# Layer 0 of two outlook-attention layers: the outer weight rows are shifted by the table's transfer instead of by TensorE

## The chip, the cores and the metric

The kernel runs on one core of one Trainium2 chip. The metric is the device time of one execution in microseconds (us); lower is better. The kernel before takes 3531.84 us, the median of three runs (3530.87 to 3535.32).

The engines go by the profile's names: PE is TensorE (matmuls), PEld its weight loads, DVE is VectorE, ACT is ScalarE, POOL is GpSimd, SP is SyncE, which here only issues transfers.

## The reference

The input x is 8 images of 56 x 56 pixels with 384 channels, in float32. Two layers follow one another, each of the form x + layer(groupnorm(x)). The change touches only layer 0:

```python
v = jnp.einsum('bhwc,oc->bhwo', x, Wv)
a = jnp.einsum('bhwc,oc->bhwo', x, Wa).reshape(b, n, heads, k2, k2)
attn = jax.nn.softmax(a * d ** (-0.5), axis=-1)
out = jnp.einsum('bnhpq,bnqhd->bnphd', attn, v_unf).reshape(b, h, w, k2, c)
canvas = canvas.at[:, i:i + h, j:j + w].add(out[:, :, :, p])   # for each p = (i, j)
```

There are 12 heads and a 3 x 3 window (k2 = 9). Every pixel makes a 9 x 9 matrix of weights for each head: the softmax runs over the nine neighbours q that are read, and there are nine target positions p that the result is added to. Reading and adding together connect a pixel with the pixels up to two rows and two columns away. So per head an output pixel has 5 x 5 summed weights, each made of several attention weights that were computed at different pixels. Layer 1 is simpler (6 heads, one weight for each of nine neighbours).

## The kernel before, in words

**Tiling.** The kernel works on two images at a time (a "pair", four of them). One column of a pair is 2 x 56 = 112 pixels, one pixel for each partition (R = 112). Layer 0 runs over 4 x 56 = 224 columns; a loop step handles one column for the first stages and earlier columns for the later ones. Seven columns make a patch, and there are 32 patches.

**A column in layer 0.** `attend` computes the logits in three groups of 288 (three matmuls each), DVE subtracts the maximum (L550, L551), ACT takes the exponential (Exp, L555), DVE makes the denominators (L567 to L573; L573 also multiplies with `inside`, which is zero where a weight would leave the image), and POOL multiplies (L574). The v projection follows; ACT copies it out (L562) and issues its transfers into a table `vtab0` in DRAM. `presum`, two steps later, adds the weights of three neighbouring columns on POOL into `pre`: for each of nine (pi, qi), and for each of five column offsets f and 12 heads, one number. `fold`, three steps after `attend`, sums over rows.

**The fold.** Five row offsets e = pi - qi + 2 from 0 to 4 are wanted. A weight that was computed at row r belongs to another row, one up or one down, when qi is 0 or 2. So `fold` multiplies `pre` with `shift[:, qi, :]`, a 112 x 112 matrix of zeros and ones that moves each row by one, once for qi = 0 and once for qi = 2, into a PSUM tile `pw` of 5 x 60 numbers. Each matmul takes all three pi at once, 180 columns. Offset e = 0 has one term only (pi 0, qi 2), and e = 4 one term only (pi 2, qi 0); for both ACT copies `pw` to the tile `wt` (L619). For e = 1, 2, 3 DVE adds the unshifted qi = 1 part (L620). Then ACT issues one transfer of `wt`, 112 partitions x 5 rows of 84 numbers, into a table `ztab0` (L625); for four of seven columns the column belongs to two patches, and there are two transfers. `wt` exists twice and `pre` twice.

**The patch.** After the last column of a patch, SP fetches the table `ztab0` and the v table back in another layout (`z` and `vp`). Four steps later PE contracts them (`pc`, L664 copies them out on ACT), then multiplies with the output weights (`po`). These come as jobs that are slipped between a column's matmuls, so of seven columns two have contractions, three have output projections and two have neither.

**What sets the order.** PE's and some others' instructions are kept in program order. The framework's scheduler sets the order of the rest, ACT's and DVE's above all, when the program is built. [...] Before a table is first used, `clear_weights` fills its margins with zeros (SP, L201).

Of the kernel before, what the change touches and what calls it, by code (L numbers as in the profile page):

```python
# [9 lines left out]
AF = mybir.ActivationFunctionType  # L10
# [5 lines left out]
def two_outlook_layers(  # L16
# [32 lines left out]
    nc = tc.nc  # L49
# [5 lines left out]
    R = IMG * H  # L55
    MARGIN = 2
# [8 lines left out]
    PX = 7  # L65
    NPX = W // PX
# [5 lines left out]
    K, K2 = 3, 9  # L72
    E0 = 2 * K - 1
# [9 lines left out]
    ROW0 = HEADS0 * PX  # L83
# [13 lines left out]
    LINE0, LINE1 = SX0 * SLOT0 + ROW0, SX1 * SLOT1 + ROW1  # L97
    NTAB = 3
# [11 lines left out]
    ztab0 = [dram.tile([RT + 1, LINE0], F32, name=f"ztab0_{n}") for n in range(NTAB)]  # L110
# [7 lines left out]
    def matmul(*args, **kwargs):  # L118
        tc.keep_in_program_order(nc.tensor.matmul(*args, **kwargs))  # L119
# [48 lines left out]
    shift = const.tile([R, K, R], F32, name="shift")  # L168
# [13 lines left out]
    inside = const.tile([R, K, PH_ALL], F32, name="inside")  # L182
# [12 lines left out]
    def fill(table, first, dims, width):  # L195

        src = zeros[: dims[0][1], :width]
        if len(dims) > 1:
            src = src.unsqueeze(1).to_broadcast([dims[0][1], dims[1][1], width])
        tc.keep_in_program_order(  # L200
            nc.sync.dma_start(bass.AP(table.tensor, table.offset + first, [*dims, [1, width]]), src)  # L201
        )
# [12 lines left out]
    def clear_weights(table, line, part, sx, slot, row, first, e, ep):  # L215
        fill(table, 0, [[part, MARGIN * line // part]], part)
        fill(table, (MARGIN + R) * line, [[part, (MARGIN + 1) * line // part]], part)
        top = MARGIN * line
        fill(table, top, [[line, R]], first * row)
        fill(table, top + (first + e) * row, [[line, R], [slot, sx]], (ep - e) * row)  # L220

    def clears():

        yield 3, lambda: clear_v(vtab0, SX0, 2)

        yield 4, lambda: fill(
            ztab0[0], MARGIN * LINE0 + FIRST0 * ROW0, [[LINE0, R], [SLOT0, 2]], E0 * ROW0
        )
        for n, t in enumerate(ztab0):
            yield (5, 2 * PX, 3 * PX)[n], lambda t=t: clear_weights(  # L230
                t, LINE0, 366, SX0, SLOT0, ROW0, FIRST0, E0, EP0
            )
        yield 4 * PX, lambda: clear_v(vtab1, SX1, 1)
        for n, t in enumerate(ztab1):
            yield (5 + n) * PX, lambda t=t: clear_weights(
                t, LINE1, 350, SX1, SLOT1, ROW1, FIRST1, K, EP1
            )
# [59 lines left out]
    def patches_of(col, pad):  # L297

        for px in range(NPX):
            sx = col - PX * px + pad  # L300
            if 0 <= sx < PX + 2 * pad:
                yield px, sx
# [94 lines left out]
    def layer0(late, pools):  # L397
# [209 lines left out]
        def fold(pair, c):  # L607


            pre = pres.pop((pair, c)).rearrange("r (pi qi) f h -> r pi qi (f h)", qi=K)  # L610
            pw = ps.tile([R, E0, E0 * HEADS0], F32, tag="f", name=f"pw_{pair}_{c}")
            for qi in (0, 2):
                matmul(
                    pw[:, 2 - qi : 2 - qi + K, :], shift[:, qi, :], pre[:, :, qi, :],
                    start=(qi == 0), stop=(qi == 2), skip_group_check=True,
                )
            wt = wts[c % NWT]
            mid = wt[:, :, SX0 - E0 : SX0, :].rearrange("r e f h -> r e (f h)")
            nc.scalar.copy(mid[:, 0 : E0 : E0 - 1, :], pw[:, 0 : E0 : E0 - 1, :])  # L619
            nc.vector.tensor_tensor(mid[:, 1 : 1 + K, :], pw[:, 1 : 1 + K, :], pre[:, :, 1, :], ALU.add)  # L620

            for px, sx in patches_of(c, 2):
                lo = SX0 - 1 - sx
                at = sx * SLOT0 + FIRST0 * ROW0
                nc.scalar.dma_start(  # L625
                    ztab0[(pair * NPX + px) % NTAB][MARGIN : MARGIN + R, at : at + E0 * ROW0].rearrange("r (e w) -> r e w", e=E0),
                    wt[:, :, lo : lo + PX, :].rearrange("r e m h -> r e (m h)"),
                )

        def fetch_v(pair, px):  # L630
# [119 lines left out]
        for step in range(NPAIR * W + LAG):  # L750
            if 2 <= step < NPAIR * W + 2:
                presum(*divmod(step - 2, W))
            todo = [lambda: jobs.run(step, 1)] * 2
            if step >= LAG:
                todo.insert(1, lambda: fold(*divmod(step - LAG, W)))
            between = lambda: todo.pop(0)() if todo else None
            if step < NPAIR * W:
                attend(*divmod(step, W), between)
                upkeep(step)
            while todo:  # L760
                between()

            pair, c = divmod(step - LAG - PX, W)
            if pair >= 0 and c % PX == 0:
                fetch_v(pair, c // PX)
            pair, c = divmod(step - LAG - PX - 1, W)
            if pair >= 0 and c % PX == 0:
                fetch(pair, c // PX, step + 4)
# [334 lines left out]
```

## Time and profile before

| what | value |
|---|---|
| median of 3 runs | 3531.84 us |
| the profiled execution, its own time | 3516.74 us |
| its span, first to last instruction | 3514.6 us |
| mean granted TensorE clock | 0.987 |
| layer 0, stretch from 75 to 2320 us | PE busy 2219.82 us, DVE 1524.10, ACT 689.01, POOL 932.48 |
| rest of the span, from 2320 us | PE busy 1155.52 of 1194.60 us |
| fold matmuls `pw` (112 x 180), 896 passes | 174.5 us busy |
| copy L619, 224 times | 58.0 us busy, 259 ns each |
| table transfers from `wt` (L625) | 336, 183.8 KB each, 6.8 us from issue to landing |

Busy time is the time in which an engine executes; issuing a transfer and waiting for a semaphore are not counted. A float32 matmul stands in the profile as two passes, so that a fold's two matmuls are four records. The durations of matmul records overlap; the distance between the starts of neighbours says what one costs. The profiled execution is one run, and the median of others lies some 15 us above it.

### The profile page before, as it was taken

The numbers are of one execution on the slowest core, as the hardware profiler recorded it, in microseconds if no ns is written. First come the engines' busy times: TensorE is split into PE (matmuls) and PEld (weight loads), VectorE is DVE, ScalarE is ACT, GpSimd is POOL, SyncE is SP. The second block draws the span as 40 slices with busy tenths as digits, with TensorE's granted clock in tenths as the row PEclk, the third lists the DMA queues.
The fourth block names the chain that finished last, engine by engine and source line by source line (L and its number), as shares of the span: only waits on it lengthen the run. The fifth ranks groups of instructions, "written<-read, shape, count | busy, mean of one in ns | idle before, by whom it ended". The sixth has DMA issues, their size and how long they took to land. (4 is left out here: it accounts for less than half of the span.)

```text
span 3514.6 us, 72311 instructions
## 1 busy us (share of the span) xinstructions
PE 3427.7 (98%) x29014; PEld 2353.0 (67%) x29014; DVE 1935.8 (55%) x4680; ACT 1173.3 (33%) x2727; POOL 1202.1 (34%) x1833
## 2 busy tenths in 40 slices
PE   7899999999999999999999999988999999999998
PEld 5577777777777777777777777655666666666665
DVE  6666666667666676667766666633333333333331
ACT  4333223333333233333322223223434434343432
POOL 2543434434344344344443444331222222221220
PEclk8999999999999999999999999999999999999998
DMA  8999988688886878887757776676878787878775
GB/s 270 286 288 282 275 275 267 212 256 253 279 263 209 272 221 273 259 252 256 236 181 226 245 225 193 222 271 192 226 221 234 217 229 219 243 205 237 216 219 147
DMA packets 672893, 839.34 MB, mean 239 GB/s; under 512 B 302190, under 2 KB 566574, under 8 KB 668462
## 3 DMA queue, kind: packets, MB, share of 16 engines
q1 hardware_dynamic: 321422, 537.46, 47.9%
q10 hardware_dynamic: 323872, 210.54, 22.7%
q0 software_dynamic: 27264, 86.73, 7.5%
q8 instruction: 228, 3.74, 0.5%
q14 instruction: 107, 0.88, 0.1%
HBM read 512.95 MB, written 321.66 MB: 237 GB/s over the span
## 5 line engine op out<-in xcount | busy, mean ns | idle before, releaser
L119 PE MATMUL bank<-wa_t,xn 128*112 128x288 f32 x4032 | 1086.9, 409 | 11.4 <-ACT v L562 7.8
L574 POOL TENSOR_TENSOR at<-at,den 112x972 f32<-112x972 f32 x224 | 504.6, 2253 | 1193.1 <-DVE den L573 1137.8
L119 PEld LDWEIGHTS bank<-wa_t,xn 128*112 128x112 f32 x4032 | 693.4, 177 | 263.7 <-issue 34.3
L119 PE MATMUL po<-yT,wo_t 128*128 128x448 f32 (+1 forms) x2304 | 817.5, 494 | 5.3 <-DVE x1t L685 4.8
L119 PEld LDWEIGHTS po<-yT,wo_t 128*128 128x128 f32 x2304 | 432.8, 191 | 293.5 <-issue 185.4
L119 PE MATMUL pc<-z,vp 121*32 121x49 f32 (+1 forms) x17664 | 487.9, 254 | 25.3 <-DMA vp<-vtab 10.4
L119 PEld LDWEIGHTS pc<-z,vp 121*32 121x32 f32 (+1 forms) x17664 | 441.3, 131 | 103.3 <-issue 79.5
L550 DVE TENSOR_REDUCE mx<-bank 112x36 f32<-112x324 f32 x672 | 327.6, 487 | 310.6 <-PE bank L119 303.7
L317 POOL DMA_DIRECT2D vtab<-v x392 | 213.1, 547 | 825.3 <-DVE v L132 810.4
L119 PE MATMUL bank<-wc_t,xn 128*128 128x438 f32 x1176 | 478.8, 543 | 5.0 <-DMA wo_t<-in_wo 5.0
L119 PE MATMUL bank<-wv_t,xn 128*128 128x384 f32 x1176 | 417.9, 492 | 0.0
L555 ACT ACTIVATE at<-at 112x972 f32<-112x972 f32 x224 | 227.0, 1014 | 344.9 <-DVE at L551 317.6
L551 DVE TENSOR_TENSOR at<-bank,mx 112x324 f32<-112x324 f32 x672 | 328.8, 489 | 21.1 <-DVE mx L550 0.5
L119 PEld LDWEIGHTS bank<-wc_t,xn 128*128 128x128 f32 x1176 | 214.0, 191 | 174.8 <-issue 162.4
L119 PEld LDWEIGHTS bank<-wv_t,xn 128*128 128x128 f32 x1176 | 219.5, 190 | 139.6 <-issue 18.7
L619 ACT COPY wt<-pw 112x120 f32<-112x120 f32 x224 | 58.0, 259 | 654.0 <-PE pw L119 591.2
L597 POOL TENSOR_TENSOR pre<-at,at 112x108 f32<-112x108 f32 (+1 forms) x440 | 238.0, 541 | 110.4 <-DVE wt L620 96.0
L567 DVE TENSOR_TENSOR d<-at 112x432 f32<-112x432 f32 x224 | 141.7, 632 | 204.7 <-ACT at L555 204.7
L132 DVE TENSOR_TENSOR lgt<-bank,ba_t 128x54 f32<-128x54 f32 x196 | 41.7, 213 | 361.3 <-PE bank L119 361.3
L132 DVE SCALAR_TENSOR_TENSOR x1t<-po,bo_t,x1t 128x448 f32<-128x448 f32 (+1 forms) x156 | 97.7, 626 | 248.9 <-PE po L119 248.9
L664 ACT COPY yT<-pc 128x294 f32<-128x294 f32 x256 | 103.4, 407 | 368.9 <-PE pc L119 325.9
L535 ACT ACTIVATE xn<-xin,bias,scale 128x224 f32<-128x224 f32 x336 | 172.9, 566 | 67.2 <-PE bank L119 36.0
(100 smaller groups left out, 2924.6 us busy)
## 6 DMA issues: line engine op xcount, KB each, us to landing
z<-ztab SPq DMA_DIRECT2D x64, 2352.0 KB, 18.0
vp<-vtab SPq DMA_DIRECT2D x64, 1536.0 KB, 8.3
ztab<-wt ACTq DMA_DIRECT2D x336, 183.8 KB, 6.8
vp<-vtab SPq DMA_DIRECT2D x64, 945.0 KB, 12.0
xres<-xT SPq DMA_DIRECT2D x32, 1176.0 KB, 10.1
xin<-xT ACTq DMA_DIRECT2D x54, 672.0 KB, 7.3
z<-ztab SPq DMA_DIRECT2D x128, 258.4 KB, 4.5
x1t<-x SPq DMA_DIRECT2D x26, 1176.0 KB, 19.0
```

Source lines behind the costliest of these rows:

```text
L119: tc.keep_in_program_order(nc.tensor.matmul(*args, **kwargs))
L132: return lambda *args, **kwargs: tc.keep_in_program_order(op(*args, **kwargs))
L317: queue.dma_start(bass.AP(table.tensor, table.offset + first, [[line, rows], [(R + GAP) * line - PX * C, n], [1, C]],), v.unsqueeze(1).to_ ...
L535: nc.scalar.activation(to[:, i, :, rows], xin[:, i, :, rows], AF.Identity, bias=bias[:, i, b : b + 1], scale=scale[:, i, b : b + 1],)
L550: nc.vector.tensor_reduce(mx[:, pi, :], pl.rearrange("r q a -> r a q"), AX.X, ALU.max)
L551: nc.vector.tensor_tensor(at[:, pi], pl, mx[:, pi, :].unsqueeze(1).to_broadcast([R, K2, PH]), ALU.subtract)
L555: nc.scalar.activation(at, at, AF.Exp, scale=SCALE0)
L567: nc.vector.tensor_add(d4, at[:, :, 0:4], at[:, :, 4:8])
L574: nc.gpsimd.tensor_tensor(at, at, den.unsqueeze(2).to_broadcast([R, K, K2, PH]), ALU.mult)
L597: nc.gpsimd.tensor_tensor(dst, terms[0], terms[1], ALU.add)
L619: nc.scalar.copy(mid[:, 0 : E0 : E0 - 1, :], pw[:, 0 : E0 : E0 - 1, :])
L664: nc.scalar.copy(yT[:, :, :, b, rows_of], pc.rearrange("p i n y m -> p i m (n y)"))
```

## The change

The outer rows, e = 0 and e = 4, are not shifted by a matmul any more. ACT writes them into `wt` at the row where they were computed, with two activations that multiply by `inside[:, qi, 0:1]`, so that a row whose weight belongs to the next image gives zero. The transfer then puts them one row lower (e = 0) or one row higher (e = 4) in the table. It is therefore split in two: one transfer for the three middle rows, one for the two outer ones. The two matmuls take two of the three pi each, 120 columns instead of 180. In each table the two places that no transfer reaches any more, e = 0 of the first row and e = 4 of the last, are filled with zeros at the start; the function that does this serves the tables of both layers.

```diff
+        fill(table, top + first * row, [[slot, sx]], row)
+        fill(table, top + (R - 1) * line + (first + e - 1) * row, [[slot, sx]], row)
...
             for qi in (0, 2):
+                lo = qi // 2
                 matmul(
-                    pw[:, 2 - qi : 2 - qi + K, :], shift[:, qi, :], pre[:, :, qi, :],
+                    pw[:, 2 - qi + lo : 4 - qi + lo, :], shift[:, qi, :], pre[:, lo : lo + 2, qi, :],
                     start=(qi == 0), stop=(qi == 2), skip_group_check=True,
                 )
...
-            nc.scalar.copy(mid[:, 0 : E0 : E0 - 1, :], pw[:, 0 : E0 : E0 - 1, :])
+
+            for e, pi, qi in ((0, 0, 2), (E0 - 1, 2, 0)):
+                nc.scalar.activation(
+                    mid[:, e, :], pre[:, pi, qi, :], AF.Copy, scale=inside[:, qi, 0:1]
+                )
             nc.vector.tensor_tensor(mid[:, 1 : 1 + K, :], pw[:, 1 : 1 + K, :], pre[:, :, 1, :], ALU.add)
...
+                table = ztab0[(pair * NPX + px) % NTAB]
+                first = table.offset + MARGIN * LINE0 + at
+                weights = wt[:, :, lo : lo + PX, :].rearrange("r e m h -> r e (m h)")
+                nc.scalar.dma_start(
+                    bass.AP(table.tensor, first + ROW0, [[LINE0, R], [ROW0, K], [1, ROW0]]),
+                    weights[:, 1 : 1 + K],
+                )
                 nc.scalar.dma_start(
-                    ztab0[(pair * NPX + px) % NTAB][MARGIN : MARGIN + R, at : at + E0 * ROW0].rearrange("r (e w) -> r e w", e=E0),
-                    wt[:, :, lo : lo + PX, :].rearrange("r e m h -> r e (m h)"),
+                    bass.AP(
+                        table.tensor, first + LINE0,
+                        [[LINE0, R], [(E0 - 1) * ROW0 - 2 * LINE0, 2], [1, ROW0]],
+                    ),
+                    weights[:, 0 : E0 : E0 - 1],
                 )
```

## The prediction

> **What bounds the kernel now.** I read the page's totals first, then the stretches of the span, then TensorE's own waits, and last one stretch of the timeline around a fold. The totals and the queues:
>
> ```profile
> span 3514.6 us, 72311 instructions
> PE 3427.7 (98%) x29014; PEld 2353.0 (67%) x29014; DVE 1935.8 (55%) x4680; ACT 1173.3 (33%) x2727; POOL 1202.1 (34%) x1833
> ...
> q1 hardware_dynamic: 321422, 537.46, 47.9%
> q10 hardware_dynamic: 323872, 210.54, 22.7%
> ...
> z<-ztab SPq DMA_DIRECT2D x64, 2352.0 KB, 18.0
> ...
> ztab<-wt ACTq DMA_DIRECT2D x336, 183.8 KB, 6.8
> ```
>
> TensorE (PE) is the bound: 87 us of the span without a matmul. The stretches split that by layer (layer 0 is 75 to 2320 us):
>
> ```profile
> 75.00:2320.00 2245.00, 2219.82 (x19721) 1586.75 (x19719) 1524.10 (x3764) 689.01 (x1357) 932.48 (x1341) 1.00 0.79 248
> ...
> 100.00:300.00 200.00, 185.51 (x1451) 131.56 (x1450) 131.47 (x330) 62.25 (x124) 92.47 (x128) 0.97 0.96 294
> ...
> 700.00:900.00 200.00, 200.00 (x1617) 143.03 (x1616) 140.06 (x359) 63.55 (x124) 82.05 (x120) 1.00 0.85 267
> ```
>
> Columns: length, busy time of PE, weight loads, DVE, ACT, POOL, then granted clock, DMA share, GB/s. In layer 0 PE is busy for 98.9% and in the middle for all of it, at a granted clock of 1.00; only the stretch from 100 to 300 us, with DMA at 0.96, leaves it 14 us idle. So PE work taken from layer 0 is time, unless the change makes PE wait. Who makes ACT wait in the steady part, 300 to 2320 us (total, times, longest):
>
> ```profile
> ACT wt L619 <- PE pw L119: 548.6, 172, 6.3
> ACT yT L664 <- PE pc L119: 285.9, 204, 3.5
> ACT at L555 <- DVE at L551: 273.0, 120, 2.9
> ...
> ACT wt L619 <- DMA vtab<-v: 28.8, 6, 5.3
> ```
>
> ACT mostly waits for PE. Its waits for a DMA come to 79 us over all lines, up to 6.1 us each, and PE has no idle time to match. One fold in the timeline (start, length in us):
>
> ```profile
> 816.91 0.78 PE L119 MATMUL pw<-pre,shift 112*112 112x180 f32 x4
> ...
> 817.52 1.62 PE L119 MATMUL bank<-wa_t,xn 128*112 128x288 f32 x6
> ...
> 817.72 0.26 ACT L619 COPY wt<-pw 112x120 f32<-112x120 f32 x1 [2.99 <-PE pw L119]
> 818.07 0.35 DVE L620 TENSOR_TENSOR wt<-pw,pre 112x180 f32<-112x180 f32 x1
> ...
> 818.45 0.32 ACTq L625 DMA_DIRECT2D ztab<-wt  x1
> ...
> 818.80 0.27 POOL L595 COPY pre<-at 112x108 f32<-112x108 f32 x1
> ...
> 820.77 1.00 ACT L555 ACTIVATE at<-at 112x972 f32<-112x972 f32 x1
> 820.92 0.55 PE L122 MATMUL pt<-ident,xr 112*128 112x112 f32 x4
> ...
> 821.30 3.08 PE L119 MATMUL bank<-wa_t,xn 128*112 128x288 f32 x12
> ...
> 824.21 0.78 PE L119 MATMUL pw<-pre,shift 112*112 112x180 f32 x4
> ```
>
> The four passes of a fold hold PE for 817.52 - 816.91 = 0.61 us. ACT copies when they are done, DVE adds, ACT issues the table's transfer. The POOL copy at 818.80 completes pre of the *next* fold, which PE asks for only at 824.21.
>
> [...] Here the 112-column transposes start every (821.30 - 820.92)/4 = 95 ns with a load each, so a pass of 120 columns is not held up by its load. [...]
>
> **The change part by part.** The sum is against the profiled execution, 3516.7 us with a span of 3514.6; the median shown is 3531.8, 15 us higher, and I carry the difference over.
>
> *PE.* Passes of 180 columns become 120. Rate: 12 passes of 288 columns from 821.30 to 824.21 are 242.5 ns each; with 95 ns for 112 columns that is 0.838 ns a column, so 120 columns take 102 ns. A fold goes from 0.61 to 0.41 us: 0.20 x 224 = 45 us less. If the weight load did hold the pass at the 176 ns that one takes, nothing is gained; the transposes exclude that.
>
> *ACT, outer rows.* One PSUM copy of 259 ns becomes two activations of 60 elements: [...] 0.57 us for both. That is 0.3 us x 224 = 69 us more, on an engine at 689 us of 2245. They wait for pre (POOL), not for PE.
>
> *ACT, issues.* 336 more ztab transfers, each about 0.35 us of ACT's queue (two in a row start 0.35 us apart): 118 us. Packets and bytes stay: 112x5 rows of 336 B become 112x3 and 112x2. The DVE add is unchanged. SP gets 12 small zero fills, of which six lie in layer 0's tables, near the first columns: hidden behind four steps that a patch waits anyway.
>
> *Order.* The built program shows the real edit. In 171 of 224 columns ACT now does the outer rows of fold c, the transfers of them and the middle transfer of fold c-1 *ahead of* Exp of column c+2; before, the copy of c-1 stood there. So a loop closes within one column: Exp (1.02), the denominators on DVE (2.8 bare, about 3.2 with what the new order puts between), POOL's multiply and pre (3.46 from den to pre), the two activations (0.57 and 0.1 of hand-over), two or four issues (0.7 or 1.4), the next Exp. Sum 9.1 us for a column with one table, 9.8 with two (four of seven columns). PE's column is 9.95 us now (224 folds from 82.5 to 2311.5 us) and 9.75 after. The loop just fits on average but not in the two columns of each seven without contraction or projection, about 7.3 us long. From the trace: Exp starts a median 1.2 us after that pre, and needs 1.45 to 2.15 (activations and issues, taken high). It would be late in 57 of the 168 such columns past the start, by 1.6 us on average. Behind it in ACT stand the v copy and xt; behind its result d (L567) in DVE, and then the reduction that frees the bank which the v matmul wants: PE can bear 1.2 to 2 us there in the short columns, 5 to 6 in the others. Most lateness falls where the margin is 5 or more. I take 10 us of PE waits in all; ends: 0, and 57 x 1.6 = 90 if the margins held nothing.
>
> *Semaphores.* [...] 4.97 issues a column look back 8/4.97 x 9.95 = 16 us; 6.47 look back 12 us. ztab's 6.8 us fits; z's 18 does not, and neither do late ones of the others. In the trace 74 of ACT's 730 steady issues stood within the lost 3.7 us of such a wait, worth 141 us of ACT time at most; the half at vtab issues come just after Exp, where ACT goes on to wait for pre anyway. I take 8 us on PE; ends 0 and 47, a third of the 141. Early, where DMA is at 0.96, the 4 us of gain of those 20 columns is not had.
>
> *z.* The middle rows' transfer now follows the next fold's activations: pre of that fold is ready a median 2.2 us after pw starts, where DVE is done after 1.5. So the table is written some 2 us later; z lands 7 to 18 us ahead of its first contraction. Nothing. pre's buffer gets a second reader, ACT, earlier than DVE's add, which POOL waits for already (96 us): nothing.
>
> Sum: -45 + 10 + 8 + 4 = -23: 3494 for the profiled execution, **3509 us** for the median.
>
> **Rivals.** *Full gain:* ACT's slack (689 of 2245 busy) takes everything: 3532 - 45 = 3487. For it, ACT's DMA waits of up to 6 us before cost PE nothing. *Eaten:* waits equal the gain, 3532: the loop's 9.1 to 9.8 us against 9.75 leaves no room for the added semaphore waits. *Slower:* the Exp loop becomes the bound. Place: ACT between POOL's pre and the next Exp; price: each stall of ACT there (z's semaphore, the fourth issue) passes whole into den, pre and the next Exp, as POOL's and DVE's parts can't be hurried; from 0.20 us of PE wait a column on average it decides. At 0.35 us it is 78 - 45 = 33 us slower, 3565. Against it: 53 columns keep the looser order, each time resetting the loop, often at the short columns. *Memory:* DMA's share of 0.79 can't bind, no byte is added.
>
> **Chances.** Partly had (3509) 0.42, full 0.16, eaten 0.15, slower 0.27. A difference within 0.2%, 7 us, can't be told from none. The range holds all but the far slow end: 3484 to 3556; the likeliest case alone 3488 to 3522. Faster 0.58, same 0.15, slower 0.27.
>
> **What would show it.** pw matmuls of 112x120, folds of 0.41 us; ACT's 548.6 us wait for pw gone, a wait for POOL's pre in its place; more ACT waits at ztab and vtab issues. Right if PE's idle time in layer 0 grows from 25 to under 60 us; wrong if "bank" or "pw" waits for DVE or POOL grow past 70 us, or if pc waits for the yT copies that stand behind the new activations.

## The result: 0.14% faster, where 0.65% was forecast

The kernel after takes 3528.64 us (median of 20 runs, 3517.24 to 3542.70), the kernel before on the same chips 3533.18 us (20 runs, 3523.22 to 3541.42). The ratio is 0.9986, with a 95% interval of 0.9975 to 0.9998: a gain of about 5 us, within the 0.2% that count as no difference here. The forecast was -23 us. The profiled execution of after has a span of 3523.7 us, 9 us *more* than the one of before, though after is not slower in the timed runs: single executions of either kernel lie up to some 16 us from their median. So below, totals are taken from the timed ratios, and places from the traces.

The page of after, its totals, two queues, two groups of instructions (busy us, mean ns | idle time ahead of them on their engine, and what ended it) and two transfers:

```profile
span 3523.7 us, 72959 instructions
...
PE 3396.9 (96%) x29014; PEld 2309.1 (66%) x29014; DVE 1915.6 (54%) x4680; ACT 1232.1 (35%) x2951; POOL 1196.8 (34%) x1833
...
q1 hardware_dynamic: 321662, 537.49, 47.7%
q10 hardware_dynamic: 329248, 210.56, 22.3%
...
L626 ACT ACTIVATE wt<-pre,inside 112x60 f32<-112x60 f32 x448 | 133.3, 338 | 796.2 <-POOL pre L598 597.0
L570 DVE TENSOR_TENSOR d<-at 112x432 f32<-112x432 f32 x224 | 140.7, 628 | 415.0 <-ACT at L558 414.2
...
z<-ztab SPq DMA_DIRECT2D x64, 2352.0 KB
...
ztab<-wt ACTq DMA_DIRECT2D x336, 110.2 KB
```

The bytes are those of before, and so nearly is their time. PE has 31 us less busy time, and the span did not follow. The line to look at is L570: DVE, which starts the denominators there, sat idle for 414.2 us until Exp (L558, L555 before) was done. In the page of before the same wait was 204.7 us:

```profile
L567 DVE TENSOR_TENSOR d<-at 112x432 f32<-112x432 f32 x224 | 141.7, 632 | 204.7 <-ACT at L555 204.7
```

Exp comes later than before.

The stretches of after, columns as for before:

```profile
75.00:2320.00 2245.00, 2187.81 (x19720) 1541.74 (x19718) 1504.21 (x3765) 747.79 (x1581) 927.23 (x1341) 0.99 0.78 248
100.00:300.00 200.00, 179.25 (x1442) 125.45 (x1440) 125.08 (x323) 70.03 (x150) 91.95 (x125) 0.97 0.92 287
700.00:900.00 200.00, 199.28 (x1886) 141.94 (x1885) 138.27 (x361) 72.99 (x153) 78.69 (x116) 1.00 0.81 256
```

PE's idle time in layer 0 went from 25 to 57 us. In the early stretch it went from 14 to 21 us in 200, while the share of DMA fell from 0.96 to 0.92. PE's largest waits in layer 0 (75 to 2320 us; total, times, longest) say for what it stood; none of them ends with a transfer:

```profile
PE pw L119 <- POOL pre L598: 18.2, 6, 8.3
PE bank L119 <- DVE at L554: 13.6, 14, 1.4
PE bank L119 <- ACT v L565: 12.3, 9, 4.3
PE pc L119 <- ACT yT L683: 8.8, 9, 2.2
PE po L119 <- DVE x1t L704: 2.4, 2, 1.7
```

Before, these were 10.2, none, 7.8, 2.0 and 0.7 us. No single wait took the gain. POOL, DVE and ACT are each a little late, as they are when a chain that runs through all three is late. ACT's waits in the steady part (300 to 2320 us) show where that chain is tied together:

```profile
ACT wt L626 <- POOL pre L598: 574.2, 143, 7.9
ACT at L558 <- DVE at L554: 147.1, 71, 4.9
ACT yT L683 <- PE pc L119: 136.9, 85, 4.7
ACT wt L626 <- DMA vtab<-v: 96.7, 19, 6.5
ACT wt L626 <- DMA ztab<-wt: 42.8, 9, 6.6
```

Before, ACT waited 548.6 us there for PE's fold; now it waits for POOL's `pre`, ahead of Exp. The two rows of L626 that name a DMA belong to `pre` as well: of the 30 waits of L626 that are put down to a DMA in this stretch, 29 end 0.03 to 0.04 us after the POOL copy (L598) that completes `pre`, as nearly all those that are put down to POOL do. The transfers named there had landed by then. Exp's own wait for its data fell from 273.0 to 147.1 us: ACT more often gets to Exp when the data have long been there. Ahead of Exp some waits for transfers are real: in the three that are put down to a fetch of z (16.8 us in all) Exp starts 7.4, 3.7 and 5.1 us after its last data.

One such case, from the timeline of after (start, length in us):

```profile
902.66 0.27 POOL L598 COPY pre<-at 112x108 f32<-112x108 f32 x1
...
902.97 0.58 ACT L626 ACTIVATE wt<-pre,inside 112x60 f32<-112x60 f32 x2 [4.32 <-POOL pre L598]
903.43 0.49 DVE L554 TENSOR_TENSOR at<-bank,mx 112x324 f32<-112x324 f32 x1
...
907.28 0.31 ACTq L641 DMA_DIRECT2D ztab<-wt  x1
907.64 1.01 ACT L558 ACTIVATE at<-at 112x972 f32<-112x972 f32 x1 [4.09 <-DMA z<-ztab]
...
908.56 0.46 ACT L565 COPY v<-bank 128x384 f32<-128x384 f32 x1
908.68 0.61 DVE L570 TENSOR_TENSOR d<-at 112x432 f32<-112x432 f32 x1 [4.76 <-ACT at L558]
...
909.07 1.71 PE L119 MATMUL bank<-wa_t,xn 128*112 128x288 f32 x6 [0.56 <-ACT v L565]
...
912.20 2.20 PE L119 MATMUL bank<-wv_t,xn 128*128 128x384 f32 x6 [1.42 <-DVE at L554]
...
912.47 2.24 POOL L577 TENSOR_TENSOR at<-at,den 112x972 f32<-112x972 f32 x1 [8.72 <-DVE den L576]
...
915.92 0.58 ACT L626 ACTIVATE wt<-pre,inside 112x60 f32<-112x60 f32 x2 [6.47 <-POOL pre L598]
```

Exp's data are complete at 903.92 (the subtraction of 903.43), but ACT has already done the outer rows of a fold, and their transfer (L641) stands ahead of Exp in its queue; by the profile it waits until a fetch of z has landed. It goes at 907.28, and Exp at 907.64, 3.7 us late. The copy of v is late with it (PE waits 0.56 us), DVE's sums are late (PE waits 1.42 us for the bank), POOL multiplies after 8.72 us of idleness, and `pre` of the next fold is late: ACT, whose next activations need it, waits until 915.92, and the next Exp comes at 916.88. PE lost 2.0 us in this column. It saves 0.2 us in each.

### The profile page after: what moved, and what is told of

It reads as the page before. It is cut to its first block, busy times and chain, and to the rows that moved or that the text cites. A ratio compares the mean times of both kernels' runs of the same rounds, so it can differ in the third digit from the quotient of the medians.

```text
span 3523.7 us, 72959 instructions
## 1 busy us (share of the span) xinstructions
PE 3396.9 (96%) x29014; PEld 2309.1 (66%) x29014; DVE 1915.6 (54%) x4680; ACT 1232.1 (35%) x2951; POOL 1196.8 (34%) x1833
## 4 chain that ended last, share of the span: by engine, by line
PE 59%; DMA 3%; DVE 3%; issue 3%; POOL 2%; ACT 2%; ACTq 1%; POOLq 0%; SPq 0%; DVEq 0%
PE bank L119 30%; PE po L119 15%; PE pc L119 9%; PE pw L119 2%; PE pt L122 1%; POOL at L577 1%; DMA lgtab<-lgt 1%; PE bank L122 1%; ACT at L558 1%; DMA at<-lgtab 1%; DMA z<-ztab 1%; POOL pre L600 1%; DMA vtab<-v 0%; DVE d L570 0%; DVE den L575 0%
## 5 line engine op out<-in xcount | busy, mean ns | idle before, releaser
L119 PEld LDWEIGHTS bank<-wa_t,xn 128*112 128x112 f32 x4032 | 684.2, 178 | 270.7 <-issue 36.8
L119 PE MATMUL bank<-wv_t,xn 128*128 128x384 f32 x1176 | 419.9, 493 | 13.7 <-DVE at L554 13.6
L626 ACT ACTIVATE wt<-pre,inside 112x60 f32<-112x60 f32 x448 | 133.3, 338 | 796.2 <-POOL pre L598 597.0
L570 DVE TENSOR_TENSOR d<-at 112x432 f32<-112x432 f32 x224 | 140.7, 628 | 415.0 <-ACT at L558 414.2
L558 ACT ACTIVATE at<-at 112x972 f32<-112x972 f32 x224 | 226.9, 1013 | 299.8 <-DVE at L554 170.3
L132 ACT COPY ot<-pt 112x384 f32<-112x384 f32 x128 | 61.3, 479 | 389.1 <-PE pt L122 353.6
```

The source lines that it names most:

```text
L132: return lambda *args, **kwargs: tc.keep_in_program_order(op(*args, **kwargs))
L558: nc.scalar.activation(at, at, AF.Exp, scale=SCALE0)
L570: nc.vector.tensor_add(d4, at[:, :, 0:4], at[:, :, 4:8])
L626: nc.scalar.activation(mid[:, e, :], pre[:, pi, qi, :], AF.Copy, scale=inside[:, qi, 0:1])
```

## The experiments

Each ratio is to the kernel before, run on the same chip, with its 95% interval; 0.0010 is 3.5 us. "Behind the full cut" is read from the traces: how much later than in the kernel before the `pw` matmuls of a column start, plus 0.2 us for each column whose fold was already cut. It comes from one profiled execution each. At column 223 it agrees with the timed ratios within some 7 us; e5_semaphores, which costs 2 us in the timed runs, stands 5.8 us behind at column 42 and 8.8 at column 223, so differences of that size can be those of two executions.

My theory, once the result was there: the order of ACT's queue, outer rows ahead of Exp, cost the gain (the loop). The rivals: the split transfers did, by ACT's added issues or by their claims on the completion semaphores (theory B in the expectations; A is the loop); or the cut was never worth 45 us. Of these semaphores the packed trace of before shows this: the 1478 transfers that ACT and SP issue signal eight of them, 184 or 185 times each; one of them comes round after 8 issues (median; in 634 of 1470 cases after exactly 8), and 476 of the issues have a wait for the semaphore that they then signal. In the trace of after it is 1826 transfers, the same eight semaphores, and 630 such waits.

**e1_pe_cut: only PE's part, in the kernel before.**

```diff
             for qi in (0, 2):
+                lo = qi // 2
                 matmul(
-                    pw[:, 2 - qi : 2 - qi + K, :], shift[:, qi, :], pre[:, :, qi, :],
+                    pw[:, 2 - qi + lo : 4 - qi + lo, :], shift[:, qi, :], pre[:, lo : lo + 2, qi, :],
...
-            nc.scalar.copy(mid[:, 0 : E0 : E0 - 1, :], pw[:, 0 : E0 : E0 - 1, :])
+            nc.scalar.copy(mid[:, 0 : E0 : E0 - 1, :], pw[:, 1 : 1 + K : K - 1, :])
```

> The matmul cut alone: 120-column passes, outer rows copied from two middle rows of pw (so the outer weights are not the right ones), one transfer as before. Both theories expect the whole gain of 0.20 us a fold, 45 us, 3488 us (ratio 0.987), since nothing on ACT or in the transfers changes. A ratio above 0.993 would say that the cut itself is worth less than its columns.

Measured: 0.9881 [0.9867, 0.9894], 3481.37 against 3522.82 us. The cut is worth 42 us. The price of a pass was right, and the gain of the early columns is had but for 7.5 us (behind the full cut at column 42; 5.5 us at column 223).

**e2_split_only: only the split transfer, in the kernel before** (the rows stay where they are, the order of ACT too).

```diff
...
+                nc.scalar.dma_start(
+                    bass.AP(table.tensor, first + ROW0, [[LINE0, R], [ROW0, K], [1, ROW0]]),
+                    weights[:, 1 : 1 + K],
+                )
                 nc.scalar.dma_start(
-                    ztab0[(pair * NPX + px) % NTAB][MARGIN : MARGIN + R, at : at + E0 * ROW0].rearrange("r (e w) -> r e w", e=E0),
-                    wt[:, :, lo : lo + PX, :].rearrange("r e m h -> r e (m h)"),
+                    bass.AP(table.tensor, first, [[LINE0, R], [(E0 - 1) * ROW0, 2], [1, ROW0]]),
+                    weights[:, 0 : E0 : E0 - 1],
                 )
```

> The kernel before with the table transfer split in two, rows where they were, nothing else. Theory A (the loop of Exp, den, pre, outer rows, next Exp costs the gain): the order on ACT is the old one, so hardly slower, under 8 us (ratio at most 1.002). Theory B (336 more issues on the eight shared completion semaphores cost the gain): 25 to 40 us slower, ratio 1.007 to 1.011, most of it before 520 us of the span.

Measured: 1.0031 [1.0020, 1.0043]: 11 us slower, more than theory A allowed and far less than theory B asked for. In its trace all of that arises before column 42 (11.9 us later than before there, 8.9 at the end).

**e3_one_transfer: the changed kernel with the one transfer of before.** 151 of 224 columns keep the outer rows ahead of Exp.

```diff
...
                 nc.scalar.dma_start(
-                    bass.AP(table.tensor, first + ROW0, [[LINE0, R], [ROW0, K], [1, ROW0]]),
-                    weights[:, 1 : 1 + K],
-                )
-                nc.scalar.dma_start(
-                    bass.AP(
-                        table.tensor, first + LINE0,
-                        [[LINE0, R], [(E0 - 1) * ROW0 - 2 * LINE0, 2], [1, ROW0]],
-                    ),
-                    weights[:, 0 : E0 : E0 - 1],
+                    ztab0[(pair * NPX + px) % NTAB][MARGIN : MARGIN + R, at : at + E0 * ROW0].rearrange("r (e w) -> r e w", e=E0),
+                    wt[:, :, lo : lo + PX, :].rearrange("r e m h -> r e (m h)"),
                 )
```

> The changed kernel with one unsplit transfer of all five rows to where they were computed (so the outer rows are not moved). The outer rows still stand ahead of Exp in most columns (151 of 224). Theory A: still near 3525 us, ratio 0.996 to 1.000. Theory B: the gain appears, 3490 us, ratio 0.988.

Measured: 0.9930 [0.9917, 0.9944]. Without the split 25 us of the 42 are had, between the two theories: neither the order nor the split takes the gain alone.

**e4_behind_exp: the changed kernel with nothing but the order undone.** The outer rows are held behind the Exp that was issued last; no column has them ahead any more. The split stays.

```diff
-            nc.scalar.activation(at, at, AF.Exp, scale=SCALE0)
+            exps.append(nc.scalar.activation(at, at, AF.Exp, scale=SCALE0).ins)
...
-            for e, pi, qi in ((0, 0, 2), (E0 - 1, 2, 0)):
-                nc.scalar.activation(
-                    mid[:, e, :], pre[:, pi, qi, :], AF.Copy, scale=inside[:, qi, 0:1]
-                )
+            with tc.issue_after(exps[-1]) if exps else nullcontext():
+                for e, pi, qi in ((0, 0, 2), (E0 - 1, 2, 0)):
+                    nc.scalar.activation(
+                        mid[:, e, :], pre[:, pi, qi, :], AF.Copy, scale=inside[:, qi, 0:1]
+                    )
```

> The changed kernel, but the outer rows of column c are held behind Exp of column c+2 on ACT in every column, so the loop never closes within one column; all transfers as in the changed kernel. Theory A: 3490 to 3500 us, ratio 0.988 to 0.991. Theory B: no better than the changed kernel, 3520 to 3530 us, ratio 0.996 to 0.999.

Measured: 0.9904 [0.9891, 0.9918], against 0.9986 of the changed kernel, as theory A expected: with the split in place, the order costs 29 us. DVE's waits from 300 to 2320 us show it, in the kernel before

```profile
DVE mx L550 <- PE bank L119: 265.0, 304, 3.2
DVE d L567 <- ACT at L555: 178.9, 98, 3.7
```

in the changed kernel

```profile
DVE d L570 <- ACT at L558: 356.5, 149, 8.5
DVE mx L553 <- PE bank L119: 148.9, 213, 2.8
```

and in e4_behind_exp:

```profile
DVE mx L553 <- PE bank L119: 240.8, 305, 5.2
DVE d L570 <- ACT at L558: 205.0, 125, 10.5
```

With the order undone DVE waits again mostly for PE's logits, as it did in the kernel before.

**e6_one_behind: both undone**, e3_one_transfer with the hold of e4_behind_exp (the two diffs above together). What is left of the change are the short matmuls and ACT's two activations.

> Outer rows from pre held behind Exp as in the run before, and the transfer unsplit (so the outer rows are not moved): loop and split both gone, the two activations left. If order and split are the whole loss: as the matmul cut alone, 0.9881 within 0.0015. If ACT's added work costs by itself: above 0.991.

Measured: 0.9896 [0.9881, 0.9912], at the edge of what was expected if order and split are the whole loss, and near e1_pe_cut (0.9881): ACT's added 75 us of activations cost some 5 us, which the intervals don't tell from nothing. With it the four corners are complete, as us gained from their ratios (each within some 5 us):

| | outer rows behind Exp | outer rows ahead of Exp |
|---|---|---|
| one transfer | 37 (e6_one_behind) | 25 (e3_one_transfer) |
| split transfer | 34 (e4_behind_exp) | 5 (the changed kernel) |

The loop alone costs 12 us, the split alone 3 us (11 us in e2_split_only), both together 32 us. The two don't add up: together they cost 17 us more than their sum, beyond the noise of some 10. That fits a loop without room, which each issue that ACT makes or waits for between `pre` and Exp lengthens; the runs show the surplus, not each stall's share in it.

**e5_semaphores and e8_act_issues: what of the split costs.** Both are the kernel before with a 16-byte transfer added beside each of the table's 336. e5_semaphores issues it from SP:

```diff
+                tc.keep_in_program_order(nc.sync.dma_start(marks[marks_n[0] : marks_n[0] + 1, :], zeros[:1, :4]))
+                marks_n[0] += 1
```

> The kernel before plus one 16-byte transfer issued by SP beside each of the 336 table transfers: as many more claims on the eight completion semaphores as the split makes, but no time of ACT's queue and no bytes. If the split's cost is the semaphores' look-back: 8 to 12 us slower before 520 us of the span and little after, ratio 1.002 to 1.0035. If it is ACT's issue time or the smaller transfers: within 3 us, ratio 0.999 to 1.001.

Measured: 1.0005 [0.9997, 1.0013]. e8_act_issues issues the same from ACT:

```diff
-                tc.keep_in_program_order(nc.sync.dma_start(marks[marks_n[0] : marks_n[0] + 1, :], zeros[:1, :4]))
+                tc.keep_in_program_order(nc.scalar.dma_start(marks[marks_n[0] : marks_n[0] + 1, :], zeros[:1, :4]))
```

> The kernel before with 336 added transfers of 16 bytes, as in e5_semaphores, but issued by ACT right behind each of the table's transfers instead of by SP. The order of ACT's activations stays that of before. ACT thus issues as often as with the split, while the table's transfers stay whole. If the split in e2_split_only (1.0031) cost because of the time and the waits of 336 more issues in ACT's queue, this run costs the same, 1.002 to 1.004. If it cost because the table's transfers themselves are cut in two, it costs no more than e5_semaphores, 1.000 to 1.001.

Measured: 1.0034 [1.0021, 1.0046], the cost of e2_split_only, with the table's transfers whole and its order of activations that of before. In its trace that too arises before column 42 (13.4 us there, 10.3 at the end). So 336 more issues in ACT's queue are enough for the whole cost; it doesn't take halved transfers, and the claims on the eight semaphores by themselves, which SP makes as often in e5_semaphores, don't make it. Not told apart is the time of ACT's issues from the waits for semaphores that ACT itself then stands in. The rows of ACT's waits that name a DMA can't settle it: in the kernel before, 12 of the 13 such waits of L619 in layer 0 end 0.04 us after the `pw` matmuls, so that most of their time is no cost of a transfer.

**e7_late_start and e10_tight_late: where the loss arises.** e7_late_start is e4_behind_exp, except that the first 42 columns fold the old way, with one transfer (`fold_all` is the fold of before; the zero fills are left out too):

```diff
+            if pair == 0 and c < OLD_WAY:
+                return fold_all(pair, c)
...
+        OLD_WAY = 42
```

> Outer rows behind Exp and split transfers, but the first 42 columns, where DMA is at 0.9, keep the old fold with one transfer, and the zero fills are left out (the old fold writes those places). The split's early loss of 10 us should go and 0.2 us be gained from column 42 on: 182 x 0.2 = 36 us, ratio 0.988 to 0.990, faster than the 0.9904 of the version without this by 0 to 8 us.

Measured: 0.9891 [0.9874, 0.9908], 3481.19 against 3525.75 us. e10_tight_late is the same without the hold, so that from column 42 on the changed kernel's order rules, as the diff of e4_behind_exp taken back:

> e7_late_start (0.9891), without the hold behind Exp: the first 42 columns of pair 0 fold the old way, with one transfer; from there on the changed kernel's order, in which ACT does the outer rows ahead of Exp in 149 of 182 columns. The starts of the folds in the traces say that the changed kernel loses 28 us against the full gain before column 42 and 19 us after it, and e7_late_start next to nothing after it. If that holds, the tight order costs this kernel about 19 us over e7_late_start: 0.9945, with 0.993 to 0.996. If the changed kernel's loss belongs to the early stretch alone, where the DMA queues are full, it comes to 0.989 to 0.991; if the early stretch only shifted what the loop costs anyway, to 0.997 or more.

Measured: 0.9938 [0.9925, 0.9952]. The loop in the later 182 columns costs 0.0047, 17 us; the trace says 17 us as well, from 2.6 us behind the full cut at column 42 to 19.5 at column 223 (20 if the 3 us that e7_late_start gains there are counted). DVE's wait for Exp (300 to 2320 us) follows, in e10_tight_late

```profile
DVE d L567 <- ACT at L555: 308.5, 138, 5.6
```

and in e7_late_start:

```profile
DVE d L567 <- ACT at L555: 179.4, 120, 4.5
```

From the changed kernel to e10_tight_late it is another 0.0048, 17 us, for the first 42 columns. e10_tight_late keeps the old fold there and so forgoes 8 us (42 x 0.2); against the full cut the early loss is 25 us. So some 60% of the changed kernel's loss is early, and the rest late, which is what its trace says:

| behind the full cut, us | column 42 | column 223 |
|---|---|---|
| the changed kernel | 27.9 | 47.3 |
| e1_pe_cut | 7.5 | 5.5 |
| e3_one_transfer | 11.7 | 15.7 |
| e4_behind_exp | 18.1 | 14.5 |
| e6_one_behind | 11.2 | 7.0 |
| e10_tight_late | 2.6 | 19.5 |
| e7_late_start | 1.1 | -1.8 |

After column 42 the kernels with the outer rows behind Exp lose nothing. With them ahead and the split transfer (the changed kernel, e10_tight_late) 17 to 19 us are lost; with them ahead and one transfer 4 us, which two executions can differ by. Whether e7_late_start is faster than e4_behind_exp can't be told from the ratios, whose intervals overlap.

**e9_outer_by_sp: e4_behind_exp with the outer rows' transfer issued by SP.**

```diff
-                nc.scalar.dma_start(
+                nc.sync.dma_start(
                     bass.AP(
                         table.tensor, first + LINE0,
```

> e4_behind_exp (0.9904), with the transfer of the two outer rows issued by SP instead of ACT. If ACT's added issues are what is left between e4_behind_exp and e6_one_behind (0.9896), this comes to 0.9885 to 0.9897. If SP's queue, which fetches z and the v tables and must now wait for ACT's activations, becomes the late one, it is slower than e4_behind_exp: 0.992 or more. A result near 0.990 tells nothing of either.

Measured: 0.9925 [0.9909, 0.9942], 7 us slower than e4_behind_exp in the ratio, with intervals that overlap a little. That is the size that was expected if SP's queue becomes the late one. SP's waits from 75 to 520 us:

```profile
SPq L642 <- ACT wt L627: 79.5, 17, 28.4
```

SP stands up to 28.4 us at the new issue (L642) until ACT has written the outer rows. By column 7 the fold is 16.0 us behind the full cut, by column 223 19.2: again a loss of the start only. Here nothing was gained by moving ACT's issues to SP.

## Why the prediction was wrong

**PE's cut: right.** In the timeline of after the `pw` matmuls start at 900.83 and the next group at 901.24: 0.41 us, as forecast. e1_pe_cut gives 42 us for 45 less the early part.

**ACT's work: right in price, and nearly free.** The profile of after gives 338 ns for one activation and 0.58 us for the pair at 902.97, where the forecast had 0.57 us for both; no such pair was in the trace of before, so that the forecast did not rest on a measurement. The traces of before and after have 17 table loads on ACT each (ACT_TABLE_LOAD). ACT's new activations take 75 us more than the old copy (133.3 - 58.0), where 69 were forecast. e6_one_behind lies 0.0015 from e1_pe_cut, which can't be told from nothing.

**The Exp loop: the step that failed, by its size.** The loop was seen, with its members, its length of 9.1 to 9.8 us against a column of 9.75, and with "each stall of ACT there" passing whole into the next Exp. Then the sum said "I take 10 us of PE waits in all". Measured are 29 us (changed kernel against e4_behind_exp), 12 only when there is no split. What was wrong is the sum's form: loop 10, semaphores 8 and the early stage 4 were three terms, each worked out as if the others were absent. The loop's lateness was counted from lengths without a stalled issue, 57 columns by 1.6 us, and covered by PE's margin; the stalls of issues were counted in another term, at places where ACT "goes on to wait for pre anyway". But that waiting for `pre` is part of the loop, and a stall ahead of Exp delays the next `pre` too. The column at 902 us is this case: one stall of 4 us, and PE lost 2.0 us, the saving of ten columns. (The two short columns of each seven were read as 7.3 us both; from fold to fold they are 7.3 and 8.8 us, medians, in the trace of before.)

**The early stage: failed by its size too.** 4 us were forecast. The changed kernel is 27.9 us behind the full cut at column 42, of which e1_pe_cut has 7.5 as well. The timed pair (changed kernel and e10_tight_late) puts the early loss at 25 us. The forecast reckoned only with a gain that isn't had where DMA's share is 0.96; it didn't ask what added issues cost there. The table's transfers take a median of 8.3 us to land up to 520 us and 6.1 us after it, in the kernel before (8 and 32 transfers, those whose landing the trace gives); that issues stall longer for that reason is not shown. e2_split_only, which adds only issues, loses 12 us there in its trace. The 29 us of the loop and these 25 us are two cuts through the same loss: by the traces of the changed kernel and e4_behind_exp some 10 us of what the order costs lie before column 42 (27.9 against 18.1) and 23 after it.

**Semaphores: about the right size, by another road.** 8 us were forecast, and the split costs 3 to 11 us in the loose order. But the argument was that ACT and SP would come round to the same of the eight semaphores after 12 us in place of 16, with 6.47 issues a column in place of 4.97 (the traces of before and after have 4.97 and 6.53), and would stand there until the transfer that used it last had landed. How long an issue stands for that reason was my estimate; no run measured it. e5_semaphores adds the same claims from SP and costs 0.05%; e8_act_issues adds them from ACT and costs 0.34%. What counts here is on which queue the added issues are made. And the lines that the forecast read for these stalls, ACT's waits at L619 for vtab, were no such stalls: all six between 300 and 2320 us end 0.04 us after the `pw` matmuls, as the copy's other waits do. A wait on the issuing queue is seen in the column at 902 us (Exp 3.7 us late) and in SP's 28.4 us of e9_outer_by_sp.

**z, the second reader of `pre`, the fills:** no wait of PE for z stands among its waits in layer 0; z mattered otherwise, as the transfer that ACT's issue stood behind, by the profile (16.8 us ahead of Exp from 300 to 2320 us). The fills weren't taken alone. e2_split_only, which has none, loses its 12 us early without them.

**The marks.** "Right if PE's idle time in layer 0 grows from 25 to under 60 us" came out as 57 us, with the gain gone all the same. The mark was badly drawn: 45 us saved less 32 us of more idle time would leave 13, but layer 0 ended 2.7 us *later* than before (the last fold, 2313.6 against 2310.9 us). The missing 15 us stand in the records as busy time: the logits' and v's matmuls take 5.6 and 2.0 us more in sum (means of 410 and 493 ns in place of 408 and 492). About as much goes with the granted clock: from 75 to 2320 us the trace of after has stretches at a clock of 0.5 that add up to 27 us, that of before 14 us, and at half speed the difference is worth up to 7 us. One of them, with its time, PE's busy time and the clock (third number from the end):

```profile
335.49 3.22 PE L119 MATMUL bank<-wa_t,xn 128*112 128x288 f32 x6 [4.26 <-ACT v L565]
...
335.20:338.60 3.40, 3.11 (x6) 1.67 (x6) 3.37 (x10) 0.68 (x2) 0.00 (x0) 0.50 1.02 341
```

Six passes take 3.22 us here and 1.62 us at 901.24, where the clock is full. PE had just waited 4.26 us; another such stretch, at 1475.2 us, comes with a wait of 1.95 us. Whether the waits lower the clock is not shown. The rest of the 15 us can't be attributed. Of the marks of being wrong, `bank` and `pw` waiting more than 70 us for DVE or POOL did not come (13.6 and 18.2 us); `pc` waiting for the yT copies behind the new activations did, with 8.8 us where it had been 2.0.

**The rivals.** Eaten is what happened, by the loop that was named under Eaten and Slower, though its stalls did not pass whole: of 3.7 us in the column at 902 us PE lost 2.0. At its point of decision, 0.20 us of PE wait a column, the loss is 45 us. In the timed runs it was 37 us (42 less 5), or 0.17 us a column.

## What to carry to other kernels

When work is given to an engine that has slack on average, look at where it lands in that engine's queue: ahead of an instruction that its own input depends on, one turn earlier, it closes a loop, and a stall of that queue can be handed on to the next turn, as the 3.7 us at 902 us were in part: PE lost 2.0 us. Cost a loop and the issues inside it as one length against the period, not as separate terms that are each hidden by the same slack. Here holding the new work behind Exp gave back 29 us (0.9904 in place of 0.9986), and with the first 42 columns left in the old form as well the change is worth 0.9891 [0.9874, 0.9908], the best ratio of a version that computes the whole result, though not told apart from 0.9904.

## What had not been expected of the hardware

336 transfers of 16 bytes each cost 1.0005 [0.9997, 1.0013] when SP issued them and 1.0034 [1.0021, 1.0046] when ACT did: some 36 ns of the kernel's time for each issue on ACT (12 us / 336), and none that can be measured on SP. In the trace all of that came in the first 42 of 224 columns. And PE's idle time understated what PE lost: 32 us more of it against 47 us of delay at the last fold, by the traces of before and after. Up to 7 us of the difference went with stretches at a clock of 0.5, one of them right behind a stall of PE; there the profile counts PE as busy.
